# Expert gates kept on chip, gating moved to ScalarE, gamma and beta folded into an eviction, and smaller second convolution matrices

## The chip, the cores and the metric

The kernel runs on one core of a Trainium2 chip. The time is device microseconds of that core, from the first to the last instruction: before the change 5471.53 us, the median of three runs (5470.37 to 5481.27). The profiled run has a span of 5461.1 us.

## The reference, cut to what matters

Input is x (32 images, 128 channels, 56 x 56), fp32. Two blocks follow each other. The first is a depthwise 7 x 7 convolution, a layer norm over channels and a mixture of 8 experts; the second works with Fourier transforms and is not touched by the change.

```python
x = conv_depthwise_7x7(input) + dw_bias                 # NHWC from here, T = 32*56*56 = 100352 tokens
x = (x - mean(x)) / sqrt(var(x) + 1e-6) * ln_gamma + ln_beta
logits = x @ Wg + bg                                     # 8 experts
topv, topi = top_k(logits, 2); wts = softmax(topv)
order = argsort(-wts[:, 0])                              # tokens by the weight of their first expert
# in this order every token asks for a place at its two experts; each takes cap = 15680
h = gelu(tokens_of_expert @ W1 + b1); y = h @ W2 + b2
contrib = y[slot] * gate                                 # gate: the token's weight at this expert
out = input + x + layer_scale * (sum of its two contribs)
```

## The kernel before, in words

The program is written with a layer that records operations per engine, puts each engine's instructions in an order of its own (by an estimate of their costs and dependences) and adds the waits. Engines take their instructions in that order. All DMAs issued from SyncE and ScalarE take turns at eight completion semaphores, and a DMA waits for the one that held its semaphore before.

**Conv stage** (lines 113 to 342). Eight groups of four images. A group has 16 steps of 8 channels (`conv`, lines 124 to 149). A step loads the tile `xt` (112 partitions, 7168 bytes each; 3 buffers) and the matrices `wt` (112 partitions, 4096 bytes: 8 channels, two matrices of 64 columns each; 3 buffers). The convolution of a block of 8 x 8 pixels is two accumulating matmuls, one for the block's own rows and one for the rows below (line 136). The second matrix is zero in its last 28 rows, since only 6 rows of pixels below the block are reached. VectorE evicts with the bias into `y` (line 144), which holds 98 tiles of 128 tokens x 128 channels. `y` has two buffers.

Behind the convolution of a group, the six phases of `block` run over the tiles of the group before, in blocks of 16 tiles: `stats` (VectorE), `norm` (ScalarE, line 181, one instruction a tile, in place), `affine` (VectorE, line 187, times gamma `gB`, plus beta `bB`, in place; then ScalarE issues the store of the block to `xf` in DRAM, line 190), `across` (TensorE transposes the tiles, line 198; ScalarE copies them to `yT`, line 200), `logits` (line 208), and `back` (line 222, logits to tokens). `BEHIND` (line 314) says how many conv steps after its block's first one each phase stands, and `plan` puts them behind the steps. When all of a group is there, `choose` (line 254) finds the two best experts, the weights, and the key by which tokens are ranked. It writes three numbers a token (both weights and the first expert) with 13 zeros into `meta` and stores it beside the token's row: a row of `xf` is PITCH = 144 floats, of which 128 are the token and 16 `meta` (line 301, 64 bytes a row).

**Expert stage** (lines 344 to 795). For each expert, `search` finds by bisection over the keys the threshold that leaves `cap` tokens (VectorE counts, line 419; TensorE sums over partitions, line 448). `listing` then makes the list of the tokens' numbers in SBUF: it ranks, computes for each token how far it has to move to the left, and moves in ten passes, one for each bit of the distance (`move`, lines 603 to 612, five VectorE instructions over 912 int16). `values` (line 621) makes numbers of them, and `collect` (line 634) turns them with 8 fp32 matmuls, 16 records in the trace, into `ids`. The first search and listing stand alone; those of the next experts are cut into steps and called by `tick` within the chunks of the expert before.

An expert has 31 chunks of up to 512 tokens. `fetch` (line 665), one chunk ahead in the text, gathers the rows by `ids` from `xf` with GpSimd's indirect DMA (line 674; four a chunk; 4 buffers `xg`), transposes them (line 680), copies them to `xT` (line 694), and makes the gates out of the three numbers that came with the row (lines 685 and 693, VectorE). `expert` (line 704): four products with W1 (line 708), each followed by a gelu on ScalarE (line 711); 16 products with W2 (line 718); VectorE adds b2 (line 731) and multiplies with the gate (line 737); SyncE stores to `yf` (line 744).

**Last stage** (from line 798): rows of `xf` are read again (line 848), both experts' rows gathered from `yf` with indirect DMAs (line 853, 1568 of them), summed, and the second block computed.

Of the kernel before, what the change touches and what calls it, by code (L numbers as in the profile page):

```python
# [52 lines left out]
PK = P8 * (P8 + 6)  # L54
CB = 8
PITCH = 144
# [15 lines left out]
def conv_seq_kernel(ctx: ExitStack, tc: tile.TileContext, t: dict, out: bass.AP, dbg: dict):  # L72
# [29 lines left out]
    xf = dram.tile([J * 128, PITCH], F32, name="xf")  # L102
# [8 lines left out]
    firsts = [rk.tile([128, J], F32, name=f"first{r}") for r in (1, 2)]  # L111

    TG = 2 * NP
    with tc.tile_pool(name="a1", bufs=1) as a1, tc.tile_pool(name="a2", bufs=2) as a2, tc.tile_pool(
# [4 lines left out]
        bB = load(a1, "bB", [128, C], rowbc(t["ln_beta"], 128))  # L119
        wg = load(a1, "wg", [C, 32], t["Wg"])  # L120
# [3 lines left out]
        def conv(g, c0, y):  # L124

            xt = a3.tile([PK, CB, 4 * NCB * NB], F32, name="xt")
            nc.sync.dma_start(out=xt, in_=t["x8"][g, c0 // CB])
            wt = a3.tile([PK, CB, 2, P8 * P8], F32, name="wt")
            nc.sync.dma_start(out=wt, in_=t["wt"][c0 // CB])
            xv = xt.rearrange("k c (h n q) -> k c h n q", h=2, n=2)  # L130
            for c4 in range(0, CB, 4):
                ps = bank("psa")
                for c in range(4):
                    for b in range(2):
                        for h in range(2):
                            nc.tensor.matmul(  # L136
                                ps[h * 64 : (h + 1) * 64, c * TG : (c + 1) * TG],
                                lhsT=wt[:, c4 + c, b, :],
                                rhs=xv[:, c4 + c, h, :, b * NB : b * NB + NP],
                                start=(b == 0),  # L140
                                stop=(b == 1),
                            )
                cs = slice(c0 + c4, c0 + c4 + 4)
                nc.vector.tensor_tensor(  # L144
                    out=y[:, :, cs],
                    in0=ps[:, : 4 * TG].rearrange("p (c t) -> p t c", c=4),
                    in1=dwbB[:, cs].unsqueeze(1).broadcast_to([128, TG, 4]),
                    op=ALU.add,
                )

        def block(g, y, lg, t0, n):
# [32 lines left out]

            def affine():
                for w, op in ((gB, ALU.mult), (bB, ALU.add)):
                    nc.vector.tensor_tensor(  # L187
                        out=yb, in0=yb, in1=w.unsqueeze(1).broadcast_to([128, n, C]), op=op
                    )
                nc.scalar.dma_start(out=xfv[:, g * TG + t0 : g * TG + t0 + n, :C], in_=yb)  # L190

            def across():
                made["yT"] = []
                for i0 in range(0, n, 4):
# [5 lines left out]
                    nc.scalar.copy(yT[:, : ni * 128], pt[:, : ni * 128])  # L200
# [51 lines left out]
            return [stats, norm, affine, across, logits, back]  # L252

        def choose(g, lg):
# [34 lines left out]
            meta = a1.tile([128, TG, PITCH - C], F32, name="meta", tag="meta")  # L289
            nc.gpsimd.memset(meta, 0.0)  # L290
            w1, w2 = meta[:, :, 0], meta[:, :, 1]
# [6 lines left out]
            nc.vector.tensor_copy(w1, m1)  # L298
            nc.vector.tensor_tensor(out=w2, in0=e1, in1=m1, op=ALU.mult)
            nc.vector.tensor_copy(meta[:, :, 2], firsts[0][:, cut])  # L300
            nc.scalar.dma_start(out=xfv[:, cut, C:], in_=meta)
# [12 lines left out]
        BEHIND = 0, 1, 3, 4, 5, 6  # L314
# [48 lines left out]
    with tc.tile_pool(name="b1", bufs=1) as b1, tc.tile_pool(name="b2", bufs=2) as b2, tc.tile_pool(  # L363
# [115 lines left out]
        def listing(e, ids):  # L479
# [5 lines left out]
            rank = b2.tile([128, J], F32, name="rank")  # L485
# [104 lines left out]
            bit = b2.tile([128, WV], I16, name="bit")  # L590

# [9 lines left out]
            steps += [sums, rowsums, ranks, kept, before, starts, starts2, shifts]  # L601

            def move(k):
# [8 lines left out]
                )  # L612

# [4 lines left out]
            val = b2.tile([128, U * 128], F32, name="val")  # L618
            hot = b2.tile([128, U, NC], F32, name="hot")

            def values():
# [6 lines left out]
                if WV < U * 128:  # L628
                    nc.vector.memset(val[:, WV:], 0.0)
                nc.vector.tensor_scalar(  # L630
# [3 lines left out]
            def collect():  # L634
                pi = bank_["i"] = rbank("pid")
                for u in range(U):
                    nc.tensor.matmul(
                        pi[:, :NC],
                        lhsT=val[:, u * 128 : (u + 1) * 128],
                        rhs=hot[:, u, :],  # L640
                        start=(u == 0),
                        stop=(u == U - 1),
                    )

            def done():
                nc.vector.tensor_copy(ids, bank_["i"][:, :NC])

# [17 lines left out]
        def fetch(e, ids, c0):  # L665

            ns = min(512, cap - c0 * 128)
            xg = c4.tile([128, 4, PITCH], F32, name="xg")
            xT = c2.tile([C, 512], F32, name="xT")
            gates = []  # L670
            pt = bank("pxt")
            for q in range(-(-ns // 128)):
# [7 lines left out]
                nc.tensor.transpose(pt[:, q * 128 : q * 128 + n], xg[:n, q, :C], ident[:n, :n])  # L680
            gate = c4.tile([128, 4], F32, name="gate")
            gat2 = c4.tile([128, 4], F32, name="gat2")
            for n, q in spans(ns):
                for to, i, op in ((gate, 0, ALU.is_equal), (gat2, 1, ALU.not_equal)):
                    nc.vector.scalar_tensor_tensor(  # L685
                        out=to[:n, q],
                        in0=xg[:n, q, C + 2],
                        scalar=float(E - e),
                        in1=xg[:n, q, C + i],
                        op0=op,  # L690
                        op1=ALU.mult,
                    )
                nc.vector.tensor_tensor(out=gate[:n, q], in0=gate[:n, q], in1=gat2[:n, q], op=ALU.add)
            nc.vector.tensor_copy(xT[:, :ns], pt[:, :ns])
            return ns, xT, gate
# [8 lines left out]
        def expert(e, c0, ns, xT, gate, tick):  # L704
            hT = c2.tile([C, FF // C, 512], F32, name="hT")
            for f in range(FF // C):
# [4 lines left out]
                nc.scalar.activation(hT[:, f, :ns], ph[:, :ns], AF.Gelu, bias=b1t[:, e, f : f + 1])  # L711
                if f % 2:
                    tick()
            py = bank("py")
# [14 lines left out]
            for n, q in spans(ns):  # L729
# [7 lines left out]
                nc.vector.tensor_tensor(  # L737
                    out=yo[:n, q],
                    in0=yo[:n, q],
                    in1=gate[:n, q].unsqueeze(2).broadcast_to([n, nq, C]),  # L740
                    op=ALU.mult,
                )
                at = row0 + q.start * 128
                nc.sync.dma_start(
                    out=yf[at : at + nq * n, :].rearrange("(q p) c -> p q c", p=n), in_=yo[:n, q]
                )

        def idtile():
            return b2.tile([128, NC], I32, name="ids")

        ids = idtile()
# [6 lines left out]
        steps, late = listing(0, ids)  # L758
# [3 lines left out]
        now = fetch(0, ids, 0)  # L762
        pairs = {0: (1, 1), 1: (2, 2), 2: (4, 2), 3: (6, 2)}
        for e in range(E):
# [3 lines left out]
            if e + 1 < E:  # L768
                ids2 = idtile()
                steps, late = listing(e + 1, ids2)  # L770
# [10 lines left out]
            for i, c0 in enumerate(chunks):  # L781
                if i + 1 < len(chunks):
                    then = fetch(e, ids, chunks[i + 1])
                elif e + 1 < E:
                    then = fetch(e + 1, ids2, 0)
                expert(e, c0, *now, tick)
                now = then
            assert state[1] == len(todo)
            if e + 1 < E:
                ids = ids2  # L790
# [53 lines left out]
    def gather(r):  # L844
# [3 lines left out]
        nc.sync.dma_start(out=xs, in_=xfv[:, r * NB : (r + 1) * NB, :C])  # L848
# [377 lines left out]
def layouts(np, v):  # L1226
# [34 lines left out]
    def bn(v, g, b, m, bias):  # L1261
# [5 lines left out]
        "wt": wt.reshape(C // CB, PK, CB, 2, P8 * P8),  # L1267
# [44 lines left out]
```

## Time and profile before

| stretch | from, to (us) | length |
|---|---|---|
| conv stage, group 0 | 12 to 92 | 80 |
| group 1 | 92 to 193.8 | 101.8 |
| groups 2 to 7 | 193.8 to 869.4 | 112.1 to 113.2 each |
| tail of the last group, up to its key | 869.4 to 970.3 | 100.9 |
| first search and listing, up to `ids` | 970.3 to 1106.9 | 136.6 |
| 8 experts, up to the last product of line 718 | 1106.9 to 3222.5 | 2115.6 |
| last stage | 3222.5 to 5461 | 2238.6 |

The ends are starts of instructions in the trace's timeline: line 144's last eviction of each group, line 304's key, line 646's `ids`. Busy over the whole span: PE 4655.5 us (85%), VectorE 3099.2 (57%), GpSimd 2575.7 (47%), ScalarE 1845.7 (34%).

How to read the page: part 2 cuts the span into 40 slices of 136.5 us; a digit is the busy share of an engine in tenths. A row of part 5 is a group of equal instructions: line, engine, operation, output <- inputs, count | busy us, mean ns | idle time of the engine just before them and who ended most of it. The answers on waits give, for a waiting instruction and the one that released it, total us, how often, and the longest. In a timeline, the bracket at the end of a line is the idle time before it and its releaser.

### The profile page before, as it was taken

The page shows a single profiled execution, that of the slowest core. Times are in us where ns is not written, and L with a number is a line of the kernel's source. Part 1 is how long each engine was busy: PE and PEld are TensorE (multiplying, and loading weights), DVE is VectorE, ACT ScalarE, POOL GpSimd, SP SyncE. Part 2 cuts the span into 40 slices and gives each one's busy share as a digit, 9 for nine tenths or more (in the row PEclk, how much of TensorE's full clock was granted, in tenths as well). Part 3 has the DMA queues.
Part 4 walks back from the last instruction along what each step waited for, and adds up shares of the span by engine and source line. Part 5 has one row for each costly group of instructions (what it writes and reads, how often), then busy time and mean ns, then how long its engine had stood idle before and what let it go on. Part 6 is the DMA issues. An engine that isn't in the chain of part 4 may idle for free.

```text
span 5461.1 us, 84959 instructions
## 1 busy us (share of the span) xinstructions
PE 4655.5 (85%) x32850; PEld 3214.4 (59%) x32850; DVE 3099.2 (57%) x6927; ACT 1845.7 (34%) x3277; POOL 2575.7 (47%) x2564
## 2 busy tenths in 40 slices
PE   7677665189898989899999965899999999999998
PEld 6566654167666767677676742455555555555556
DVE  4777776746575656453544321555555555555566
ACT  1554456023232323233333320233333333333333
POOL 0000000053535344445454447777777777777770
PEclk8888887589998989999999987999999999999999
DMA  9999995222222222222222243355444444444442
GB/s 256 239 252 249 240 237 141 51 63 61 70 57 65 60 61 64 61 66 72 67 71 73 74 123 69 98 136 138 126 124 131 124 124 127 127 125 128 125 122 48
DMA packets 616212, 634.05 MB, mean 116 GB/s; under 512 B 166145, under 2 KB 540546, under 8 KB 611714
## 3 DMA queue, kind: packets, MB, share of 16 engines
q1 hardware_dynamic: 332418, 395.64, 25.5%
q0 software_dynamic: 81664, 175.18, 14.2%
q10 hardware_dynamic: 201728, 57.81, 5.5%
q8 instruction: 260, 4.26, 0.3%
q14 instruction: 142, 1.16, 0.1%
HBM read 454.98 MB, written 173.41 MB: 115 GB/s over the span
## 4 chain that ended last, share of the span: by engine, by line
POOL 26%; PE 24%; issue 19%; DVE 10%; DMA 8%; ACT 2%; ACTq 0%; DVEq 0%; POOLq 0%; SPq 0%
POOL y L853 17%; POOL xg L674 10%; PE py L718 7%; PE ph L708 5%; DMA y<-yf,slot 4%; PE pf L898 3%; DMA xg<-xf,ids 3%; PE pm L942 3%; ACT y L181 2%; PE pt L934 1%; PE psa L136 1%; DVE y L187 1%; PE pxt L680 1%; PE pyt L198 1%; DVE junk L419 1%
## 5 line engine op out<-in xcount | busy, mean ns | idle before, releaser
L853 POOL DMA_INDIRECT y<-yf,slot x1568 | 1602.6, 1022 | 530.0 <-issue 501.4
L674 POOL DMA_INDIRECT xg<-xf,ids x984 | 961.7, 977 | 1328.2 <-PE pxt L680 466.8
L711 ACT ACTIVATE hT<-ph,b1t 128x512 f32<-128x512 f32 (+1 forms) x992 | 675.8, 682 | 1416.9 <-PE ph L708 1390.6
L718 PEld LDWEIGHTS py<-W,hT 128*128 128x128 f32 x7872 | 946.5, 194 | 218.9 <-issue 147.6
L718 PE MATMUL py<-W,hT 128*128 128x128 f32 x7872 | 993.3, 281 | 69.9 <-DVE yo L731 65.5
L898 PE MATMUL pf<-xp,cw 128*64 128x448 f32 x4032 | 907.3, 565 | 0.5 <-DVE xp L880 0.5
L708 PE MATMUL ph<-xT,W 128*128 128x512 f32 (+1 forms) x1984 | 904.8, 596 | 0.4 <-DVE bn_shift L820 0.4
L708 PEld LDWEIGHTS ph<-xT,W 128*128 128x128 f32 x1984 | 360.6, 194 | 336.3 <-issue 329.1
L898 PEld LDWEIGHTS pf<-xp,cw 128*64 128x64 f32 x4032 | 287.1, 140 | 438.4 <-issue 408.5
L867 DVE TENSOR_TENSOR xs<-xs,y 128x896 f32<-128x896 f32 x224 | 244.1, 1090 | 462.8 <-DMA y<-yf,slot 385.7
L136 PE MATMUL psa<-xt,wt 112*64 112x98 f32 x8192 | 415.9, 264 | 80.0 <-DMA wt<-in_wt_dram 71.9
L685 DVE SCALAR_TENSOR_TENSOR gat<-xg 128x4 f32<-128x4 f32 (+2 forms) x256 | 42.1, 164 | 772.0 <-DMA xg<-xf,ids 771.1
L136 PEld LDWEIGHTS psa<-xt,wt 112*64 112x64 f32 x8192 | 392.3, 147 | 117.2 <-issue 65.9
L936 DVE COPY mid<-pt 112x512 f32<-112x512 f32 (+3 forms) x480 | 306.1, 660 | 263.0 <-PE pt L934 259.8
L290 POOL MEMSET meta<- 128x1568 f32 x8 | 11.2, 1404 | 881.7 <-DVE df L168 233.7
L181 ACT ACTIVATE y<-y,nb,sd 128x128 f32<-128x128 f32 x784 | 307.9, 482 | 125.4 <-issue 86.4
L144 DVE TENSOR_TENSOR y<-psa,dwbB 128x392 f32<-128x392 f32 x256 | 142.9, 562 | 223.8 <-PE psa L136 223.8
L945 ACT COPY T<-pm 128x464 f32<-128x464 f32 (+2 forms) x240 | 124.7, 519 | 392.6 <-PE pm L942 392.3
L906 ACT ACTIVATE feat<-pf,bn_shift,bn_scale 128x448 f32<-128x448 f32 x112 | 81.1, 724 | 451.9 <-PE pf L898 393.8
L731 DVE TENSOR_TENSOR yo<-py,b2t 128x512 f32<-128x512 f32 (+2 forms) x256 | 169.7, 666 | 110.3 <-PE py L718 107.9
L198 PE MATMUL pyt<-ident,y 128*128 128x128 f32 x784 | 129.6, 332 | 91.6 <-DVE nb L174 56.4
L680 PE MATMUL pxt<-ident,xg 128*128 128x128 f32 (+1 forms) x984 | 195.5, 281 | 10.4 <-DMA xg<-xf,ids 10.4
(376 smaller groups left out, 5973.3 us busy)
## 6 DMA issues: line engine op xcount, KB each, us to landing
xt<-in_x_dram SPq DMA_DIRECT2D x128, 784.0 KB
yf<-yo SPq DMA_DIRECT2D x240, 256.0 KB
xp<-in_xp_dram SPq DMA_DIRECT2D x32, 1832.0 KB
wt<-in_wt_dram SPq DMA_DIRECT2D x128, 448.0 KB
xs<-xf SPq DMA_DIRECT2D x112, 448.0 KB
xf<-y ACTq DMA_DIRECT2D x48, 1024.0 KB
y<-yf,slot POOLq DMA_INDIRECT x1568
out_dram<-oa SPq DMA_DIRECT2D x224, 112.0 KB
```

Source lines behind the costliest of these rows:

```text
L136: nc.tensor.matmul(ps[h * 64 : (h + 1) * 64, c * TG : (c + 1) * TG], lhsT=wt[:, c4 + c, b, :], rhs=xv[:, c4 + c, h, :, b * NB : b * NB + N ...
L181: nc.scalar.activation(yi, yi, AF.Identity, scale=sd[:, i : i + 1], bias=nb[:, i : i + 1])
L198: nc.tensor.transpose(pt[:, i * 128 : (i + 1) * 128], y[:, t0 + i0 + i, :], ident)
L674: nc.gpsimd.indirect_dma_start(out=xg[:n, q, :], out_offset=None, in_=xf, in_offset=bass.IndirectOffsetOnAxis(ap=ids[:n, c0 + q : c0 + q + ...
L680: nc.tensor.transpose(pt[:, q * 128 : q * 128 + n], xg[:n, q, :C], ident[:n, :n])
L708: nc.tensor.matmul(ph[:, :ns], lhsT=W1[:, e, f * C : (f + 1) * C], rhs=xT[:, :ns], start=True, stop=True)
L711: nc.scalar.activation(hT[:, f, :ns], ph[:, :ns], AF.Gelu, bias=b1t[:, e, f : f + 1])
L718: nc.tensor.matmul(py[:n, q * C : (q + 1) * C], lhsT=hT[:, f, q * 128 : q * 128 + n], rhs=W2[:, e, f, :], start=(f == 0), stop=(f == FF // ...
L853: nc.gpsimd.indirect_dma_start(out=y[:, m, :], out_offset=None, in_=yf, in_offset=bass.IndirectOffsetOnAxis(ap=s[:, r * NB + m : r * NB + ...
L867: nc.vector.tensor_tensor(out=xs, in0=xs, in1=y, op=ALU.add)
L898: nc.tensor.matmul(pf[i * DD : (i + 1) * DD, : 8 * W], lhsT=cw[:, k, :], rhs=xps[i][:, o : o + 8 * RP].rearrange("p (h w) -> p h w", w=RP) ...
L936: dve(mid[:m, :ni, :].rearrange("p i c -> p (i c)"), pt[:m, : ni * 128])
```

## The change

It has four parts.

1. **Gates on chip.** `meta` is gone; `xf` has rows of 128 floats. The second weight stays in SBUF as `w2`, the first is the key itself. `listing` carries a row of gates `gv` along with the distances: it starts as `w2`, a predicated copy puts in the key of the tokens whose first expert this is, and each of the ten moves copies under the same mask as the distances (`copy_predicated`). Eight more matmuls turn the gates into a tile `gates` beside `ids`. `fetch` makes no gates.
2. **Gating on ScalarE.** The multiplication with the gate is four ScalarE copies with a per-partition scale for a chunk. They and the store are held back and put behind the last gelu of the next chunk (`issue_after`); the last chunk's come after the loop. The sum with b2 stays on VectorE.
3. **Conv stage.** The transposes read the normalised tiles before gamma and beta; ScalarE's eviction of the transposed tile applies them as per-partition scale and bias (`gC`, `bC`). `affine` is the last phase, for the stored rows alone. `BEHIND` is shorter by one step.
4. **Second matrices on 84 partitions.** `wt` becomes two tiles and two loads, `wt0` with 112 partitions and `wt1` with 84 (2048 bytes a partition each); the second matmul reads 84 partitions of `xt`.

`rank` and `val` have one buffer instead of two.

```diff
-    xf = dram.tile([J * 128, PITCH], F32, name="xf")
+    xf = dram.tile([J * 128, C], F32, name="xf")
+    w2 = rk.tile([128, J], F32, name="w2")
...
-            wt = a3.tile([PK, CB, 2, P8 * P8], F32, name="wt")
-            nc.sync.dma_start(out=wt, in_=t["wt"][c0 // CB])
+            wts = [a3.tile([k, CB, P8 * P8], F32, name=f"wt{b}") for b, k in enumerate(PKS)]
+            for b in range(2):
+                nc.sync.dma_start(out=wts[b], in_=t[f"wt{b}"][c0 // CB])
...
-                                lhsT=wt[:, c4 + c, b, :],
-                                rhs=xv[:, c4 + c, h, :, b * NB : b * NB + NP],
+                                lhsT=wts[b][:, c4 + c, :],
+                                rhs=xv[: PKS[b], c4 + c, h, :, b * NB : b * NB + NP],
...
-                    nc.scalar.copy(yT[:, : ni * 128], pt[:, : ni * 128])
+                    nc.scalar.activation(
+                        yT[:, : ni * 128], pt[:, : ni * 128], AF.Identity, scale=gC, bias=bC
+                    )
...
-            return [stats, norm, affine, across, logits, back]
+            return [stats, norm, across, logits, back, affine]
...
-            meta = a1.tile([128, TG, PITCH - C], F32, name="meta", tag="meta")
-            nc.gpsimd.memset(meta, 0.0)
...
-            nc.vector.tensor_copy(w1, m1)
-            nc.vector.tensor_tensor(out=w2, in0=e1, in1=m1, op=ALU.mult)
-            nc.vector.tensor_copy(meta[:, :, 2], firsts[0][:, cut])
-            nc.scalar.dma_start(out=xfv[:, cut, C:], in_=meta)
+            nc.vector.tensor_tensor(out=w2[:, cut], in0=e1, in1=m1, op=ALU.mult)
...
-        BEHIND = 0, 1, 3, 4, 5, 6
+        BEHIND = 0, 1, 3, 4, 5, 5
...
+            def gating():
+                nc.vector.memset(gv[:, :128], 0.0)
+                nc.vector.tensor_copy(gv[:, 128:WV], w2)
+                if WV < U * 128:
+                    nc.vector.memset(gv[:, WV:], 0.0)
+                nc.vector.tensor_scalar(
+                    out=tie, in0=firsts[0], scalar1=float(E - e), scalar2=None, op0=ALU.is_equal
+                )
+                nc.vector.copy_predicated(gv[:, 128:WV], tie.bitcast(I32), key[:, e, :])
...
+                nc.vector.copy_predicated(gv[:, : WV - d], bit[:, d:], gv[:, d:WV])
...
+                nc.vector.scalar_tensor_tensor(
+                    out=gv[:, :WV], in0=a, scalar=0.0, in1=gv[:, :WV], op0=ALU.is_gt, op1=ALU.mult
+                )
...
+                for at, of in ((0, val), (256, gv)):
+                    for u in range(U):
+                        nc.tensor.matmul(
+                            pi[:, at : at + NC],
...
+                nc.vector.tensor_copy(gates, bank_["i"][:, 256 : 256 + NC])
...
-            xg = c4.tile([128, 4, PITCH], F32, name="xg")
+            xg = c4.tile([128, 4, C], F32, name="xg")
...
-                for to, i, op in ((gate, 0, ALU.is_equal), (gat2, 1, ALU.not_equal)):
-                    nc.vector.scalar_tensor_tensor(
...
-                nc.vector.tensor_tensor(out=gate[:n, q], in0=gate[:n, q], in1=gat2[:n, q], op=ALU.add)
...
+            with tc.issue_after(gelu.ins):
+                before()
...
-                nc.vector.tensor_tensor(
-                    out=yo[:n, q],
-                    in0=yo[:n, q],
-                    in1=gate[:n, q].unsqueeze(2).broadcast_to([n, nq, C]),
-                    op=ALU.mult,
-                )
...
+            def after():
+                for q in range(-(-ns // 128)):
+                    n = min(128, ns - q * 128)
+                    nc.scalar.activation(
+                        yo[:n, q], yo[:n, q], AF.Copy, scale=gates[:n, c0 + q : c0 + q + 1]
+                    )
```

## The prediction

> **What bounds the kernel now.** I read the page's slices first, then the sums by stretch, then the waits of each stretch. The three stages have different limits. The slices (engine PE, DMA share, GB/s):
>
> ```profile
> PE   7677665189898989899999965899999999999998
> DMA  9999995222222222222222243355444444444442
> GB/s 256 239 252 249 240 237 141 51 63 61 70 57 65 60 61 64 61 66 72 67 71 73 74 123 69 98 136 138 126 124 131 124 124 127 127 125 128 125 122 48
> ```
>
> Slices 1 to 6 (the conv stage) have the DMA engines full and PE three quarters busy; slices 9 to 23 (experts) and the last 15 have PE or GpSimd full and DMA idle enough. Sums for stretches I cut where the evictions of line 144 end a group (193.8, 306.4, 419.1 ... 869.4 in the timeline), then the tail, the first search and listing, the experts, the rest:
>
> ```profile
> core 0: us, PE busy (x) PEld busy (x) DVE busy (x) ACT busy (x) POOL busy (x), PEclk, DMA share, GB/s
> 92.00:194.00 102.00, 79.52 (x1198) 67.81 (x1198) 72.36 (x204) 56.90 (x137) 0.00 (x0) 0.88 0.98 262
> 194.00:307.00 113.00, 78.30 (x1198) 65.01 (x1198) 83.66 (x223) 58.39 (x139) 1.41 (x1) 0.89 1.02 245
> 307.00:419.00 112.00, 80.20 (x1198) 66.83 (x1198) 82.56 (x220) 58.51 (x139) 1.40 (x1) 0.88 1.02 246
> 970.00:1107.00 137.00, 25.91 (x84) 20.06 (x84) 97.88 (x255) 0.00 (x0) 0.00 (x0) 0.51 0.23 50
> 1107.00:3224.00 2117.00, 1982.54 (x11263) 1446.17 (x11262) 1099.18 (x2779) 682.78 (x999) 961.69 (x984) 0.97 0.25 66
> 3224.00:5461.00 2237.00, 1986.48 (x11920) 1195.81 (x11920) 1235.68 (x2128) 695.20 (x1166) 1602.62 (x1568) 0.95 0.46 119
> ```
>
> The first row is the key: group 1 of the conv stage stores rows, but no `meta` is under way in it; it took 101.8 us. Every later group has the `meta` of two groups back in it and takes 112.6. What stalls there (DMA queue's own waits, 136 to 819), and what the first listing waits for (timeline of VectorE):
>
> ```profile
> SPq L127 <- DMA xf<-meta: 105.3, 6, 18.5
> ```
>
> ```profile
> 986.91 0.71 DVE L473 MEMSET onesj<- 128x784 f32 x1 [14.58 <-DMA xf<-meta]
> ```
>
> The loads of `xt` stand 17.5 us behind each `meta`, and the search starts 14.6 us late behind the last one. In the expert stage (waits, 1092 to 3190) PE is the bound, with gaps:
>
> ```profile
> DVE gat L685 <- DMA xg<-xf,ids: 771.1, 224, 6.2
> POOL xg L674 <- PE pxt L680: 466.8, 147, 6.9
> PE pid L637 <- DVE val L627: 69.1, 5, 38.5
> PE py L718 <- DVE yo L731: 65.5, 28, 9.7
> ```
>
> From the timeline a chunk is 7.71 us when nothing stalls; 248 chunks are 1912 of 2117 us, PE gaps over 0.5 us make 128, the rest is the routing's matmuls. In the last stage:
>
> ```profile
> L853 POOL DMA_INDIRECT y<-yf,slot x1568 | 1602.6, 1022 | 530.0 <-issue 501.4
> ```
>
> 1568 x (1.02 + 0.31 issue) = 2085 of 2237 us: GpSimd paces it, and the change does not touch it.
>
> **What the Trainium skill says.** (1) "DMA: Bandwidth & Descriptors", Specifications: rows under 512 B do not reach line rate. The trace agrees: a `meta` is 12544 packets of 64 B, which took 18 ns each in the conv stage (9 with nothing beside them), a 512 B row 32 ns. (2) The same page, "Why a DMA increments its semaphore by 16 and not by 1": a DMA runs on the largest number of engines up to 16 that divides its partitions, so 112 takes 16 and 84 takes 14. No run yet shows it. (3) "ScalarE: Activation LUTs", "What ACT_TABLE_LOAD costs": each per-partition operand adds about 93 ns. The trace agrees: line 200's copy 586 ns, line 711 with a bias 687, both at 512 columns. (4) "VectorE: DVE Perf Modes", perf-mode tier table: two-source fp32 work goes one element per cycle; line 595 (784 elements, 966 ns) agrees.
>
> **The change part by part.**
>
> *Conv stage: `meta` gone, second matrices smaller.* Bytes of a group now: `xt` 16 x 803 kB, `wt` 16 x 459 kB, rows 6.42 MB, `meta` 0.80 MB: 27.4 MB. After: 25.7 MB. Because of the 14 engines I count the loads by the fuller engines: 76.8 instead of 78.8 kB a step each, so as if 26.1 MB. Stretches without `meta` or waits (718 to 760) move 261 to 286 GB/s; at 265 this is 98.4 us, plus 2 us of the PE stalls that group 1 shows as well: 100. VectorE is busy 83 us of that and ScalarE 58 + 25 x 0.19 (the eviction with gamma and beta: 586 + 2 x 93 = 772 ns) = 63, so both fit, VectorE with little to spare. Bounds: 96 (DMA alone) and 107. Group 0 (80 us, loads only) falls by 2.6% to 78. Sum: 2 + (101.8 - 100) + 6 x 12.6 = **-79 us**; bounds: 7 groups at 107 give -30, at 96 they give -107.
>
> *Three loads a step instead of two.* In the built order all loads and stores take turns at eight completion semaphores, so a load waits for the eighth DMA before it. Now that is over three steps back, then 2.3 steps. A step is 6.2 us, so one load is always under way: 0 us. (That `xt` waits for a `meta` at all comes from this sharing.)
>
> *Tail (869 to 970).* The transposes stop waiting for lines 187's two passes (2 x 2.28 us), but ScalarE's evictions grow, 25 x 0.19 = 5 us, and it is busy 59 of 101. In the built order the late passes still precede `choose` on VectorE. **-3**, bounds -12 to +5.
>
> *First search and listing.* The 14.6 us wait goes (no `meta`). Added to the serial chain: ten predicated copies, mean length 810. The trace has none; lower bound the int16 pass of line 608 (634 ns at 912), upper bound the scan's pace (line 559: 1.79 us at 784). I take the two-source pace: 810 x 1.04 ns + issue = 0.9, so 9.0; a compare (0.6) and a copy (0.97), of which 0.6 falls into the wait for `pst`; the new pass over 912 of line 646 1.1; 16 more records of `pid` 3.8 (16 took 3.79). The memsets and the copy of `w2` stand in the search's waits in the built order. Sum +15. **+0.5 net.**
>
> *Later listings.* The matmuls run on the bound engine: 7 x 3.8 = **+26**. On VectorE, from `pst` to `val` (1597 to 1645) it works without pause for the listings of experts 2 to 4, and PE waits 8.8, 9.6 and 10.9 us at `pid`. Added 11.6, removed six gate products (0.6 each) and some 2.6 of lines 685 and 693: +5.4 each, 3 x 5.4 = **+16**. Listing 1 and those of experts 5 to 7 are spread over more chunks (PE gap 1.4 or none): 0.
>
> *Gates off VectorE.* Lines 685 wait in VectorE's order for gathers of chunks far ahead; at each of four expert borders the eviction of line 731 stands behind them, and PE waits 7.3, 9.7, 9.4 and 9.7 us. Nothing of this is left after: -36, and of the other 31 us of small gaps at `py` I take 12: **-48**.
>
> *Gating on ScalarE.* Four copies with a per-partition scale, about 0.30 us apart (186 + 107 + 93 ns less overlap): 1.2 us a chunk on an engine busy 683 of 2117 us. Behind the new wait (for line 731's eviction) stand the next chunk's gelus; they come 3.6 us later, since PE is then in `py`. **0**; only the last store is later, **+0.7**. Gather rows of 512 instead of 576 B: the gather is behind a prefetch, 0. `rank`, `val` and `gv` have one buffer each; the writer of the next listing comes many chunks after the last reader: 0.
>
> Sum: -79 - 3 + 0.5 + 26 + 16 - 48 + 0.7 = -86.8: 5471.5 - 87 = **5385 us**.
>
> **Rivals.**
> - *The conv stage does not shorten as far.* For it: VectorE at 83 of 100 us, and PE in order, so its matmuls stand behind transposes. Against: group 1 ran at 101.8 with 72 us of VectorE. At 107 a group: +49, 5434.
> - *Predicated copies at the scan's pace.* For: unseen instruction with three operands. +9 on the first listing, three tight ones, and part of the others: +45, 5430.
> - *More than forecast.* The step of 16 us in the middle of a group (the chain of waits has ScalarE held 12 us at the issue of line 190) goes, so groups reach 96, and all gaps at `py` go: -28 - 19, 5338.
> - *Slower than before.* A load held by a semaphore of a store starves PE, so the conv stage keeps only 20 of 79 us; copies at the scan's pace (+45) and no gain at `py` (+48). Then 5385 + 59 + 45 + 48 = 5537. Against: the stores in group 1 land without holding loads.
>
> **How the numbers follow.** Forecast 0.51, conv short of it 0.14, slow copies 0.12, more 0.17, slower 0.06. The range 5325 to 5445 holds the first four with little room and leaves out the last and mixes of two bad cases. Faster by over 0.2% (below 5460.6): 0.92; within 0.02; slower 0.06.
>
> **What would show it.** Group length 100 in the evictions' times; no wait of 14 us ahead of the search's first memset; the predicated copy's mean near 0.9 us; PE's gap at `pid` near 15 us and its gap at `py` gone at the borders; the last stage still 2237. A group at 107 or more, or predicated copies at 1.8 us, makes the forecast wrong.

## The result and the profile after

The changed kernel takes 5347.66 us (median of four runs, 5338.74 to 5354.01) beside 5470.95 before: ratio 0.977, 95% interval 0.975 to 0.979. The forecast was 5385. Its profiled run has a span of 5337.0 us, 124 less than before. Three of the kernels below ran on another chip, on which the kernel before took 6459 us, with the added time behind the conv stage; of their traces only the conv stage and the gaps at `pid` are used. By stretches, cut at the same instructions as in the table of the kernel before:

| stretch | before | after | difference | forecast |
|---|---|---|---|---|
| conv stage, up to the last eviction | 869.4 | 833.8 | -35.6 | -79 |
| of it, groups 2 to 7, each | 112.6 | 107.6 | -5.0 | -12.6 |
| tail | 101.0 | 95.6 | -5.4 | -3 |
| first search and listing | 136.6 | 133.8 | -2.8 | +0.5 |
| experts | 2115.6 | 2038.5 | -77.1 | -6 |
| last stage | 2238.7 | 2235.2 | -3.5 | +0.7 |

So the sum was near, and two of its terms were far off, in opposite directions. The slices of the page of the changed kernel:

```profile
PE   7888885299989898999999956999999999999998
...
DMA  9888883121212121222222243444444454444442
```

In slices 2 to 6 PE is at 8 tenths, where it was at 6 or 7, and DMA is at 8 instead of 9. The sums by stretch of the changed kernel (groups 1, 2 and 4 of the conv stage, and the experts):

```profile
core 0: us, PE busy (x) PEld busy (x) DVE busy (x) ACT busy (x) POOL busy (x), PEclk, DMA share, GB/s
...
90.30:188.00 97.70, 83.14 (x1198) 64.65 (x1198) 74.43 (x205) 61.11 (x137) 0.00 (x0) 0.93 0.96 261
188.00:300.00 112.00, 93.97 (x1210) 71.07 (x1208) 83.65 (x221) 62.45 (x139) 0.00 (x0) 0.89 0.86 234
...
403.00:513.00 110.00, 92.31 (x1206) 69.09 (x1201) 83.50 (x221) 62.45 (x139) 0.00 (x0) 0.91 0.83 236
...
1063.00:3102.00 2039.00, 1971.39 (x11379) 1444.12 (x11377) 952.03 (x1873) 967.73 (x1980) 966.00 (x984) 0.98 0.23 64
```

DMA's share is 0.96 in group 1, and 0.83 to 0.86 in the two others, where it was 0.97 to 1.02 before. Yet those groups are longer than group 1. The expert stage has PE busy for 1971 of 2039 us, 97%.

The lines shown of the kernel before have these answers. The loads' 105 us of waiting for `meta` are gone. These are SyncE's own waits in the changed kernel, 136 to 800 us; the waiting for PE to give a buffer back was there before as well (459.2 us in the same window):

```profile
SPq L134 <- PE psa L141: 355.6, 57, 11.4
...
SPq L131 <- DMA xf<-y: 57.8, 6, 10.4
```

The second line is what the prediction named as a danger: a load that waits for the completion of a store of rows. It happens six times in 57.8 us of waiting. The first search starts without a wait (timeline of VectorE, no bracket behind the line that had 14.58 us):

```profile
931.26 0.71 DVE L475 MEMSET onesj<- 128x784 f32 x1
```

PE's waits in the expert stage, 1075 to 3050: `py` has left the list, which had 65.5 us of it, and `pid` has grown from 30.6 to 40.5.

```profile
PE pid L657 <- DVE val L643: 40.5, 4, 13.4
```

The last stage's gathers are as before, 1568 of 1024 ns (1022 before) with 524.7 us of idle time ahead of them (530.0 before).

### The profile page after: what moved, and what is told of

The parts are those of the page before. It is cut to its first block, busy times and chain, and to the rows that moved or that the text cites. A ratio compares the mean times of both kernels' runs of the same rounds, so it can differ in the third digit from the quotient of the medians.

```text
span 5337.0 us, 85251 instructions
## 1 busy us (share of the span) xinstructions
PE 4715.7 (88%) x32978; PEld 3218.8 (60%) x32978; DVE 2963.5 (56%) x6023; ACT 2163.7 (41%) x4261; POOL 2571.8 (48%) x2556
## 5 line engine op out<-in xcount | busy, mean ns | idle before, releaser
L873 POOL DMA_INDIRECT y<-yf,slot x1568 | 1605.6, 1024 | 524.7 <-issue 450.1
L141 PE MATMUL psa<-xt,wt 84*64 84x98 f32 (+1 forms) x8192 | 452.1, 269 | 87.3 <-DMA wt<-in_wt_dram 59.5
L141 PEld LDWEIGHTS psa<-xt,wt 84*64 84x64 f32 (+1 forms) x8192 | 412.2, 151 | 147.1 <-issue 50.7
L754 ACT ACTIVATE yo<-yo,gates 128x128 f32<-128x128 f32 (+1 forms) x984 | 311.4, 389 | 1.8 <-DVE yo L744 1.8
L421 DVE TENSOR_SCALAR_CACHE_REDUCE junk<-key,trial 128x784 f32<-128x784 f32 x192 | 191.9, 1027 | 3.9
L1053 PE MATMUL pim<-feat,meanw 128*128 128x448 f32 x224 | 115.4, 599 | 81.9 <-ACT gt L1107 81.9
```

The source lines that it names most:

```text
L141: nc.tensor.matmul(ps[h * 64 : (h + 1) * 64, c * TG : (c + 1) * TG], lhsT=wts[b][:, c4 + c, :], rhs=xv[: PKS[b], c4 + c, h, :, b * NB : b ...
L754: nc.scalar.activation(yo[:n, q], yo[:n, q], AF.Copy, scale=gates[:n, c0 + q : c0 + q + 1])
L873: nc.gpsimd.indirect_dma_start(out=y[:, m, :], out_offset=None, in_=yf, in_offset=bass.IndirectOffsetOnAxis(ap=s[:, r * NB + m : r * NB + ...
```

## The experiments

Stage lengths below are from the profiled run of each kernel; "groups" is the mean of groups 2 to 7. Five kernels below leave the conv stage of the changed kernel as it is; with it their groups are 106.4 to 107.8 us and their conv stages end at 831.8 to 844.6. Differences within these spreads say nothing.

### Conv stage: which part did what

Three kernels undo part 4, part 3, and both.

```diff
-            wts = [a3.tile([k, CB, P8 * P8], F32, name=f"wt{b}") for b, k in enumerate(PKS)]
-            for b in range(2):
-                nc.sync.dma_start(out=wts[b], in_=t[f"wt{b}"][c0 // CB])
+            wt = a3.tile([PK, CB, 2, P8 * P8], F32, name="wt")
+            nc.sync.dma_start(out=wt, in_=t["wt"][c0 // CB])
```

> The changed kernel with part 4 undone: one weight load of 112 partitions a step again, both matrices in it (0.92 MB a group more, two loads a step instead of three). Theory A (the load bytes bound the conv stage): a group of 107.6 us grows by 0.92 MB / 265 GB/s = 3.5 us, eight groups +28, total 5376. Theory B (PE's order of work, in which matmuls stand behind the transposes and logits of the group before, bounds it; DMA is at 0.86): groups within 2 us of 107.6, total 5335 to 5363. If three loads on the shared completion semaphores cost something (loads waiting for stores of rows, 57.8 us in the trace after), groups get shorter than 107.6 and the total falls under 5335.

```diff
-            return [stats, norm, across, logits, back, affine]
+            return [stats, norm, affine, across, logits, back]
-        BEHIND = 0, 1, 3, 4, 5, 5
+        BEHIND = 0, 1, 3, 4, 5, 6
-                    nc.scalar.activation(
-                        yT[:, : ni * 128], pt[:, : ni * 128], AF.Identity, scale=gC, bias=bC
-                    )
+                    nc.scalar.copy(yT[:, : ni * 128], pt[:, : ni * 128])
```

> The changed kernel with part 3 undone: gamma and beta on VectorE ahead of the transposes again, plain copy in the eviction, phases at their old steps. Theory A (bytes bound): conv groups stay at 107.6, tail +3 to +5, total 5348 to 5354. Theory B (PE's in-order waits bound): the chain from norm to transposes is 4.6 us longer for each block of 16, groups go to 111 to 114, total 5370 to 5400.

Both diffs together:

> Parts 3 and 4 undone together: the conv stage is that of the kernel before without meta, and the expert stage is that of the changed kernel. Theory A: groups at 26.6 MB / 265 GB/s + 2 = 102.5 (close to group 1 of the kernel before, 101.8), conv stage no longer than after, since meta was what made groups 112.6: total 5310 to 5350. Theory B: groups at 108 to 114, total 5350 to 5410. Expert stage 2039 us in both.

| kernel | time, ratio to before (interval) | conv end | groups | tail | experts |
|---|---|---|---|---|---|
| before | 5470.9 | 869.4 | 112.6 | 101.0 | 2115.6 |
| without parts 3 and 4 | 5356.8, 0.979 (0.976 to 0.981) | 842.7 | 108.1 | 103.9 | 2038.8 |
| without part 3 | 5357.2, 0.978 (0.976 to 0.980) | 844.8 | 108.3 | 103.9 | 2041.6 |
| without part 4 | 5374.0, 0.981 (0.979 to 0.983) | 864.7 | 112.6 | 97.0 | 2039.2 |
| changed | 5347.7, 0.977 (0.975 to 0.979) | 833.8 | 107.6 | 95.6 | 2038.5 |

What follows. Removing `meta` (row 2 against row 1) gave 27 of the conv stage's 36 us, 4.5 a group and not 12.6. Part 4 by itself (row 3 against row 2) gave nothing that can be seen: 3% of a group's bytes fewer, and groups 0.2 us longer, which speaks against theory A; it also shows no cost of a third load a step there, as forecast. Part 3 by itself (row 4) made groups 4.5 us longer and the tail 7 us shorter. With part 4 beside it, its loss in the groups is gone. That interaction none of the theories had: without both parts theory B was met, without part 3 neither was, and without part 4 the total met theory A's 5376, though row 3 contradicts its reason. In the kernel without part 4 PE waits for `wt` twice as long (51.9 us from 200 to 800, instead of 25.3); why the order with early transposes and one large load starves it was not settled.

A rival for the small differences is PE's granted clock. Over groups 2 to 7 it was 0.87 before, 0.88 in row 2, 0.87 in row 3, 0.89 in row 4 and 0.92 in the changed kernel, and within the changed kernel a group of 103.7 us had 0.95 and one of 111.5 had 0.89. Whether a lower clock makes a group longer here, or a group with more waiting is granted a lower clock, no run separates.

### Conv stage: are the loads what sets a group?

The weights of step 0 are loaded once and used by every step:

```diff
+        wts = [a1.tile([k, CB, P8 * P8], F32, name=f"wt{b}") for b, k in enumerate(PKS)]
+        for b in range(2):
+            nc.sync.dma_start(out=wts[b], in_=t[f"wt{b}"][0])
+
         def conv(g, c0, y):
...
-            wts = [a3.tile([k, CB, P8 * P8], F32, name=f"wt{b}") for b, k in enumerate(PKS)]
-            for b in range(2):
-                nc.sync.dma_start(out=wts[b], in_=t[f"wt{b}"][c0 // CB])
```

> The changed kernel without the weight loads of the steps: the weights of step 0 are loaded once and used by all steps (so the convolution's values are wrong); 6.4 MB of 25.7 MB a group are gone, and every step has one load. Theory B (loads and PE's stalls add up): groups under 95. Theory C (PE's order alone): groups 104 to 108. In both the first group falls to 50 to 60, since it is loads only.

5303.4 us in a single run; groups 105.6, conv end 794.1 (more than half of the difference in group 0, which is loads only). The sum over 105 us, a group's length, of this kernel:

```profile
core 0: us, PE busy (x) PEld busy (x) DVE busy (x) ACT busy (x) POOL busy (x), PEclk, DMA share, GB/s
...
293.00:398.00 105.00, 87.76 (x1201) 64.88 (x1200) 83.00 (x219) 62.48 (x140) 0.00 (x0) 0.92 0.68 185
```

DMA is down to two thirds, and a group still takes over 105 us, with PE busy for 88: a quarter of the stage's bytes is gone, and a group is 0.8 to 2.2 us shorter than with all loads. So the bytes do not set a group of the changed kernel. What is left is PE's own work and what it waits for in its order. Five load buffers instead of three, which would have let the loads run further ahead, do not fit (55 KB a partition, 45.4 free), so that this was not measured.

VectorE is the other candidate. Its two passes of gamma and beta over the stored rows are left out:

```diff
             def affine():
-                for w, op in ((gB, ALU.mult), (bB, ALU.add)):
-                    nc.vector.tensor_tensor(
-                        out=yb, in0=yb, in1=w.unsqueeze(1).broadcast_to([128, n, C]), op=op
-                    )
                 nc.scalar.dma_start(out=xfv[:, g * TG + t0 : g * TG + t0 + n, :], in_=yb)
```

> The changed kernel without the two VectorE passes of gamma and beta over the rows that are stored (the rows stored lack gamma and beta); VectorE's work in a group falls from 83 to 52 us. If VectorE, which has to evict the conv banks in between, is what keeps groups at 107.6, they go to 100 or less and the tail loses some 5 us or more: total 5290 or less. If PE's order and the loads set them, they stay within 3 us: total 5325 to 5345.

Groups 103.6, conv end 811.7, tail 94.0, 5315.6 us in a single run. VectorE's work from 300 to 520 us falls from 171.9 to 128.5, and a group gives only 2.8 to 4.2 us: between the two expectations. VectorE is in the way now and then, but does not set the group.

### Conv stage: can PE's order be bettered?

In the changed kernel the four logits matmuls of a block, which lie beside each other in the PE array and run at once, are parted by the built order. PE's timeline, group 5:

```profile
547.66 1.05 PE L216 MATMUL plq<-yT,wg 128*32 128x512 f32 x2
...
549.46 1.04 PE L216 MATMUL plq<-yT,wg 128*32 128x512 f32 x2
...
579.96 1.07 PE L216 MATMUL plq<-yT,wg 128*32 128x512 f32 x8
```

A logits matmul is two records. Eight records that stand together take 1.06 or 1.07 us in 15 of 20 cases in the changed kernel (the other five take 2.1 to 3.9), and two take 1.04 us between other matmuls. Two kernels with other steps for the phases put them together again:

```diff
-        BEHIND = 0, 1, 3, 4, 5, 5
+        BEHIND = 0, 1, 3, 5, 6, 6
```

> The changed kernel with the logits of a block, and what follows them, one conv step later (steps 0, 1, 3, 5, 6, 6 instead of 0, 1, 3, 4, 5, 5). In the built order the four logits matmuls of a block then stand together; in the changed kernel they are taken apart into pairs with transposes between. Theory L (PE's own order sets the group: logits in pairs take 14.8 instead of 10.2 us of PE a group, and PE waits 5.6 us a group for the yT they read): groups from 107.6 to 98 to 103, total 5285 to 5320. Rival (the waits of PE only move on to the next thing it stands behind): groups stay at 105 to 108, total 5335 to 5355.

```diff
-        BEHIND = 0, 1, 3, 4, 5, 5
+        BEHIND = 0, 1, 3, 5, 7, 6
```

> As the run with the logits one step later, and with two steps instead of one from the logits to the transposes back (0, 1, 3, 5, 7, 6), whose wait for lq is 3.6 us of PE a group in the changed kernel. Theory L: groups 3 us shorter again, 95 to 100, total 5265 to 5300. Rival: groups at 105 to 108, total 5335 to 5355.

Both ran on the other chip, where a kernel with the conv stage of the changed one had groups of 107.8. Groups: 107.6 and 115.0 (totals 6410.6, ratio 0.992, and 6460.0, ratio 1.000). For the first the rival was right; the second is worse than both theories allowed. PE's waits of the changed kernel and of the one with the logits one step later, 200 to 800 us:

```profile
PE plq L216 <- ACT yT L206: 28.6, 11, 3.9
...
PE pl L230 <- ACT lq L225: 21.7, 12, 2.3
```

```profile
PE pl L230 <- ACT lq L225: 63.9, 21, 7.6
```

The logits' 28.6 us of waiting for `yT` went, and the wait for `lq` went from 21.7 to 63.9 us. In the second kernel the wait for `lq` is gone, and the transposes wait 44.7 us for ScalarE's `norm`. I counted the time from each matmul's start to the next in groups 2 to 7, up to 0.6 us as work and the rest as waiting; a wait shorter than that hides in the work (us a group):

| kernel | work | of it logits | waiting | group |
|---|---|---|---|---|
| before | 83.3 | 10.4 | 28.8 | 112.6 |
| without parts 3 and 4 | 84.5 | 9.9 | 23.3 | 108.1 |
| changed | 92.6 | 14.7 | 14.7 | 107.6 |
| logits one step later | 87.7 | 6.4 | 19.5 | 107.6 |
| and transposes back another step later | 101.9 | 6.7 | 12.6 | 115.0 |
| weights loaded once | 90.6 | 14.8 | 14.7 | 105.6 |
| no gamma and beta for rows | 91.6 | 14.5 | 11.9 | 103.6 |

So parts 3 and 4 took 8.6 us of waiting from a group and put 8.1 us of short intervals in its place: 4.8 of the logits and 4.3 of the convolution's matmuls, less 1.0 of the others. Of the 4.3 us, 3.9 go again when the weights are loaded once, so they look like short waits for loads. The kernel that waits least is the slowest: its transposes have 27.5 us of short intervals instead of 18.5 in the kernel above it, and the convolution 63.5 instead of 58.3; why was not settled. The waits of the kernel without parts 3 and 4, 200 to 800 us, and one of them:

```profile
PE pyt L203 <- DVE nb L178: 67.2, 12, 9.6
PE pl L227 <- ACT lq L222: 37.5, 16, 3.6
```

```profile
548.94 3.59 PE L203 MATMUL pyt<-ident,y 128*128 128x128 f32 x16 [6.73 <-DVE nb L178]
```

The name in the profile is that of the instruction that happened to end last, `nb` of a later block. Each of these twelve waits ended 0.15 us after the second pass of `affine` over the block that was to be transposed (548.79 for the one shown), and 4.8 us or more after the last `norm`. So the transposes stood 67.2 us behind gamma and beta on VectorE, which part 3 takes out of their way. In the changed kernel they are parted into pieces between other matmuls and no longer wait, and so are the logits, which pay for it.

### Experts: the gaps at `py`, and the move to ScalarE

```diff
+                nc.vector.tensor_tensor(
+                    out=yo[:n, q],
+                    in0=yo[:n, q],
+                    in1=gates[:n, c0 + q.start : c0 + q.stop].unsqueeze(2).broadcast_to([n, nq, C]),
+                    op=ALU.mult,
+                )
             def after():
-                for q in range(-(-ns // 128)):
-                    n = min(128, ns - q * 128)
-                    nc.scalar.activation(
-                        yo[:n, q], yo[:n, q], AF.Copy, scale=gates[:n, c0 + q : c0 + q + 1]
-                    )
```

> The changed kernel with the product with the gate on VectorE as before (one tensor_tensor of 512 columns right behind the bias eviction, out of the gates tile), the store still behind the next chunk's gelus. Theory A (PE's gaps at py came from VectorE waiting for gathers ahead to read gates from them): no gaps at py; VectorE has 0.67 us a chunk more, which lengthens the three tight listings by about 3 us each: +9 us, total 5357. Theory B (the gaps came from VectorE being too full): gaps at py come back, +40 to +70 us, total 5390 to 5420.

5353.1 us, ratio 0.978 (0.975 to 0.980); experts 2056.2, no gap over 0.5 us at `py`. PE's wait at `pid` in this kernel, 1075 to 3050:

```profile
PE pid L657 <- DVE val L643: 57.6, 4, 17.5
```

Theory A holds: the gaps at `py` came from gates read out of rows that were still on their way, and they are gone with the product on either engine. The move to ScalarE is worth 17.7 us of the stage, 17.1 of it at `pid` (57.6 instead of 40.5): the gap grows by 4.1 to 4.6 us in each of four listings, where I expected 3 in three of them. In whole runs the two kernels cannot be told apart.

### Experts: what the predicated copies cost

```diff
-                nc.vector.copy_predicated(gv[:, : WV - d], bit[:, d:], gv[:, d:WV])
```

> The changed kernel without the ten predicated copies of each listing (the gates stay where their tokens are, so most gates are wrong); they have 1.05 us each by the trace after. By the prediction's step: the first listing loses 10 us, and the three tight listings lose 10 us each of the PE gaps at pid, which are then 0 to 3 us: together 40, total 5305 to 5312. If the gaps at pid come from something else than the length of VectorE's chain, only the first listing gains: total 5335 to 5340.

5298.4 us, ratio 0.966 (0.965 to 0.968). First listing 129.1 us, 4.7 us shorter than in the changed kernel and up to 7.5 shorter than in others with the same listing (133.8 to 136.6); experts 31.6 us shorter; PE's wait at `pid`:

```profile
PE pid L656 <- DVE val L642: 13.8, 3, 5.0
```

The step holds: what is taken from VectorE's chain comes off PE's wait at `pid`, 26.7 us (1.8 of them in the listing of expert 1) beside the 3 x 10.7 us that the tight listings' copies take. The first listing gave less than the 10.6 us of its ten copies; the cause is open.

### Experts: is the chain too long, or only placed too late?

Experts 2 and 3 search for pairs that are needed two experts later, and the listing that is needed at once stands behind:

```diff
-            if e in pairs:
-                todo = todo + search(*pairs[e])
+            more = search(*pairs[e]) if e in pairs else []
+            if e < 2:
+                todo = todo + more
             if e + 1 < E:
                 ids2, gates2 = lists()
                 steps, late = listing(e + 1, ids2, gates2)
                 todo = todo + steps
+            if e >= 2:
+                todo = todo + more
```

> The changed kernel with the work of experts 2 and 3 on VectorE in another order: the listing of the next expert (which needs only thresholds found an expert earlier) ahead of the search for the expert after it, instead of behind. Theory P (the PE gaps at pid of experts 3 and 4, 13.4 us each, come from the listing's chain, with its ten predicated copies, standing at the end of its expert behind a search): two of the three gaps go, PE gaps at pid 40.6 to about 14, total 5320 to 5325. Rival (VectorE is too full in these experts whatever the order): the wait only moves to pn or py, total 5340 to 5355.

On the other chip 6325.3 us, ratio 0.979; `pid` gaps 14.7 us, as theory P has it, but the total says nothing there. The same kernel once more:

> The same kernel as in the run with the listings of experts 3 and 4 ahead of the searches, once more, because the chip of that run was 18% slower with the kernel before as well; there PE's gaps at pid fell from 40.6 to 14.4 us. Theory P: expert stage 2039 to about 2012, total 5317 to 5325. Rival (VectorE is too full, the wait moves to pn or py): expert stage 2030 to 2040, total 5340 to 5355.

5301.8 us, ratio 0.966 (0.965 to 0.968); experts 1999.5. PE's wait at `pid`:

```profile
PE pid L657 <- DVE val L643: 15.1, 4, 12.0
```

39 us off the stage, where 27 were expected, and the total is below theory P's range. `pid` gave 25.4 of them, and the wait of transposes for gathered rows (`pxt`) fell from 15.4 to 6.8; 5 us are in PE's own records. Then expert 1, too:

```diff
-        pairs = {0: (1, 1), 1: (2, 2), 2: (4, 2), 3: (6, 2)}
+        pairs = {1: (3, 1), 2: (4, 2), 3: (6, 2)}
...
+            if e < 2:
+                todo = todo + search(e + 1, 1)
```

> As the run above, and for expert 1 the search for experts 2 and 3 together is parted: search 2, listing 2, search 3. Theory P: the last tight gap (12.0 us at the listing of expert 2) falls to 2 or less, as at the listing of expert 1 (1.8); 25 more pn matmuls cost PE about 6 us; pid gaps about 4, net -4 to -6 against the run above, total 5311 to 5321. If a listing is tight for another reason than standing behind a search of two, the gap at expert 2 stays near 12 and the total rises by 6.

5287.7 us, ratio 0.965 (0.964 to 0.967); experts 1991.8. Theory P again, with a total below its range since the run above lay below its own:

```profile
PE pn L450 <- DVE junk L421: 9.6, 22, 2.3
PE pid L657 <- DVE val L643: 2.6, 3, 1.8
```

The last tight gap is gone; waiting at `pn` takes back 5 us of it (9.6 instead of 4.7), and the stage is 7.7 us shorter. The intervals of the two kernels overlap, but both lie below the changed kernel's. This kernel beats before and after: it keeps the whole change and gives the listings their time.

## Why the prediction was right, and where it was not

The time was in the range, the direction right, and 5385 is 0.7% above the measured 5347.7. By its steps:

- **`meta` gone and smaller matrices, -79: wrong, -35.6.** The term that failed is "At 265 this is 98.4 us, plus 2 us of the PE stalls that group 1 shows as well: 100". It lets the bytes set the group, and has PE's stalls at 2 us. The runs show the opposite: with the weights loaded once a group loses 2.2 us at most, and PE waits 14.7 us in a group of the changed kernel, on top of 92.6 us of work and short waits. 107.6 lies outside the term's bounds of 96 and 107, and "A group at 107 or more" is what the prediction itself named as a sign of being wrong. The answer from which it took the line on `meta` (136 to 819 us) has another line above that one:

```profile
SPq L127 <- PE psa L136: 471.4, 90, 14.4
```

  The loads stood far longer for PE to give a buffer back than for `meta`. And PE itself, from 136 to 800 us of the kernel before, waited less for loads than for its order:

```profile
PE pyt L198 <- DVE nb L174: 55.7, 11, 9.8
PE pl L222 <- ACT lq L217: 46.6, 16, 5.9
PE plq L208 <- ACT yT L200: 41.1, 8, 7.6
PE psa L136 <- DMA wt<-in_wt_dram: 41.0, 26, 2.6
```

  The 2 us came from group 1 at 101.8, read as a group that lacks only `meta`. But without `meta`, and with nothing else changed in the stage, the later groups took 108.1 and group 1 104.4. In the changed kernel group 1 takes 97.9 and the later ones 107.6. Group 1 also has no finished group for `choose`; VectorE is busy 74 us in it and 83 in the others. VectorE's and PE's timelines at the start of group 5:

```profile
516.70 0.57 DVE L149 TENSOR_TENSOR y<-psa,dwbB 128x392 f32<-128x392 f32 x1
...
523.89 1.48 DVE L306 TENSOR_TENSOR key<-hot,top 128x784 f32<-128x784 f32 x1
...
527.33 0.55 DVE L149 TENSOR_TENSOR y<-psa,dwbB 128x392 f32<-128x392 f32 x1
```

```profile
521.44 7.71 PE L141 MATMUL psa<-xt,wt 112*64 112x98 f32 x128 [4.78 <-DVE hot L281]
```

  From 516.70, when one conv bank is evicted, to 527.33, when the next is, VectorE works mostly through the choosing of the group two back. The profile puts PE's wait of 4.78 us down to it. But that matmul waits for two loads as well; the later of them had landed at 521.30, 0.14 us before it started, while the last eviction was done at 517.27. So PE waited for a load, and then ran on while VectorE was still choosing. What makes the later groups longer than group 1 is open; that it is `choose` is not shown.

  Part 4 gave nothing by itself, and bytes do not set the time. The eviction with gamma and beta took 772 ns, as priced. The Trainium skill, "TensorE: Matmul & The Clock Gate", Step-by-step: what each phase is for, says that the time of a weight load goes by its columns, not by its rows. The trace agrees, 148 ns with 84 rows and 147 with 112, and shows the same of the matmuls (mean ns behind the comma):

```profile
L141 PE MATMUL psa<-xt,wt 112*64 112x98 f32 x3148 | 302.4, 266 | 48.0 <-DMA wt<-in_wt_dram 26.6 <-DMA xt<-in_x_dram 11.8 <-DVE hot L281 4.8
L141 PE MATMUL psa<-xt,wt 84*64 84x98 f32 x3152 | 301.8, 265 | 4.5 <-DMA wt<-in_wt_dram 3.9
```

  How many DMA engines the load of 84 partitions took, no run here shows.
- **Three loads a step, 0: right** where it could be read alone (108.3 against 108.1).
- **Tail, -3: -5.4**, in the bounds. Part 3 alone gave -8.3 (103.9 to 95.6), and the rest of the change took 2.9 back.
- **First search and listing, +0.5: -2.8** in this trace; eleven other kernels with the same stretch took 133.9 to 136.6 us, so between -2.8 and 0. The wait of 14.6 us went as said. Predicated copies are 1.0 to 1.2 us at most lengths, not 0.9; with the one that puts in the keys (the sum's "a copy (0.97)") there are eleven in a listing, 11.6 us for 10.0. The second eight matmuls were 1.95 us, not 3.8: the 3.79 us had been read where the granted clock was half (0.51 in the prediction's sums), and the first eight took 3.71 us at 0.50 again, the second eight 1.95 at 1.00:

```profile
L628 DVE COPY_PREDICATED gv<-bit,gv x80: 596/1150/1229, 1018.1 to 2771.3; 128x911 f32<-128x911 int16 x8, 128x910 f32<-128x910 int16 x8, 128x908 f32<-128x908 int16 x8, 128x904 f32<-128x904 int16 x8
...
L613 DVE COPY_PREDICATED gv<-tie,key x8: 1020/1048/1081, 1010.6 to 2695.4; 128x784 f32<-128x784 int32 x8
```

```profile
1057.73 3.71 PE L657 MATMUL pid<-hot,val 128*128 128x123 f32 x16 [48.24 <-DVE val L643]
1061.28 1.95 PE L657 MATMUL pid<-hot,gv 128*128 128x123 f32 x16
```

- **Later listings' matmuls, +26: about +15**, 1.95 us each in four listings and 2.2 to 2.8 in the three that follow a long wait at `pid`, where the granted clock was lower.
- **Tight listings, +16: +10** at `pid`. The gap expected at 15 us is 12.0 and twice 13.4. The mechanism is as said; the experiments on the moves and on the order show it.
- **Gates off VectorE, -48: -66.8.** The borders' gaps went, and all of the small ones too; I had allowed 12 of 31. Beside that, three terms that the sum did not have: PE's gaps at `pn` fell by 10.0 and at `pst` by 4.9, those at `pxt` rose by 9.3. Records of `py`, `ph` and `pxt` were shorter by 18 us in all (281 to 278 ns for `py`), at a granted clock of 0.98 instead of 0.97. With +10 and +15 this makes -65 of the stage's -77; 12 us, in gaps under 0.5 us and in records, I did not trace.
- **Gating on ScalarE, 0: more.** It does nothing to PE directly, as forecast (four copies took 1.26 us), but against the same product on VectorE it is worth 17 us at `pid`.
- **Last stage, +0.7: -3.5.** The pace of the gathers is unchanged. The first one starts 4.5 us behind the last product instead of 10.1; in SyncE's timeline the last stores of `yf` now stand ahead of the first load of `xp` (1832 KB) and not behind it.

Of the rivals, the first came true in its number (groups at 107) and in part in its mechanism (PE in its order, though behind logits and loads more than behind transposes), and half of the third did (all gaps at `py` go). At 5434 and 5338 they were on either side. That the forecast was near is luck: the conv stage gave 43 us less than its term and the experts 71 us more than theirs.

## What to carry to other kernels

When a part of the load on a bound resource is taken away, what is left is found by the next limit, and an undisturbed stretch of the old trace shows it only if it lacks nothing else: compare which operations it holds before its length is used, and ask whether the issuing queue waits for the engine that is fed. On an engine that runs in order, a phase moved to an earlier or later step can trade one wait for another, as both moves did here; sum work and waits for the whole period before and after. Check the releaser that a profile names against what the instruction needs: twice here it was an instruction that happened to end at the same time. A list that is needed at the end of a period belongs ahead of work that is needed a period later; here that alone took 39 us off, at the same work for VectorE.

## What the runs showed of the hardware

- Four 32-column matmuls at 512 columns took 1.07 us together where nothing held them, and one of them alone among other matmuls 1.04 us, at full granted clock. The Trainium skill, "TensorE: Matmul & The Clock Gate", Part 3: Packing small matmuls — row/col tiling, says that such tiles run at once; that another matmul between them costs the whole gain, these records show.
- A predicated copy of fp32 under an int16 mask took 1.20 us in the mean at 911 columns and 0.60 us at 400; at 784 columns it took 1.03 us under an int16 mask and 1.05 us under an int32 one. The pass with two tensors and a scalar beside it (`scalar_tensor_tensor`) took 1.10 us at 912 columns.
